# A selective-scan layer over image lines: step-size stores in slot 1, the gate behind the next turn's first scan, and another spread of B's units over VectorE and GpSimd

## The chip, the core and the metric

The kernel runs on one core of a Trainium2 chip. Times are device microseconds (us) of that core. The engines are TensorE (PE; its weight loads are listed as PEld), VectorE (DVE), ScalarE (ACT), GpSimd (POOL) and SyncE (SP), whose queue issues all the DMAs. Each engine works through its own queue in the order of the program, and waits for the others by semaphores.

## The reference, cut to what matters

Four residual layers follow one another on eight images of 48 x 48 pixels with 96 channels: a scan over the whole image in four directions (layer 0), a spectral layer (1), a scan over single lines in four directions (2, "lines"), and a second scan over the whole image (3). The change is in the lines layer, and in one helper that the two image scans also call. For each of its four directions lines computes

```python
xz = x @ in_w
xi = silu(conv4(xz[..., :192]) + conv_b)        # causal, 4 taps along the line
dt_low, Bm, Cm = split(xi @ xproj_w, [6, 22])
dt = softplus(dt_low @ dt_w + dt_b)             # step sizes
h = exp(dt * A) * h + (dt * xi) * Bm            # per channel and state, 16 states
y = (h * Cm).sum(states) + D * xi
y = y * silu(xz[..., 192:])                     # the gate
out += y @ outp_w @ out_w
```

with 192 inner channels in two halves of 96. A line is 48 pixels, and h starts from zero on each.

## The kernel before

**Blocks, slots, turns.** Each image and direction is cut into five blocks of lines: four of 10 lines (480 columns) and one of 8 (384 columns). Lines has 8 x 4 x 5 = 160 blocks. In a block there are 192 x 16 = 3072 pairs of channel and state, which lie on 128 partitions as 24 units of one block's columns each. Eight slots of three units make up the block: slots 0 to 3 belong to channel half 0, 4 to 7 to half 1, in the state order 0 1 2 3 3 2 1 0 (`ORDER`), so that slot 3 and slot 4, 2 and 5 and so on share B and C. Two slots make a turn; a block has four turns, q = 0 to 3, with at = 2 * (turn number).

**One turn in `scans`** (the loop from line 377), per engine in program order:

- DVE: `scan` of units 0 and 1; `make_dbu(at + 2)`, the product of dt * xi with B for the units of a slot of the *next* turn that lie on DVE; `scan` of units 2 and 3; `make_dbu(at + 3)`; `scan` of units 4 and 5; then `finish(at + 1)`.
- POOL: `make_hc(t - 1, 1)`, the product of the states with C for the second slot of the turn before; the units of `make_dbu(at + 2)` and `(at + 3)` that lie on POOL; `make_hc(t, 0)`.
- ACT: `make_da` (exponentials into PSUM, two buffers, two units each), `copy_b` of B for slots at + 3 and at + 4 into the one PSUM buffer that DVE reads, and what the block's preparation needs.
- PE: `reduce(t - 1, 0)` and `reduce(t - 1, 1)`, which sum over the states into the tile y. y has one PSUM bank. The first reduction of a half begins with an "opening" matmul that writes D * xi there, so it needs the bank free. After the last of a half, the pair (block, half) goes into the list `ends`.

`aside(at)` and `aside(at + 1)` stand in the middle and at the end of the turn. They issue, in this order, the loads of bc (B and C, slots 2, 3, 6, 7, for the next block) and of dd (step sizes dt and products dt * xi, slots 3 and 5, one channel half each, for the next block), a piece of side work, the preparation steps of `stage1` for later blocks, and the steps in `later`.

`finish` takes what lies in `ends` and calls `done` for it (line 838): DVE multiplies y by silu(z) into `gated` (the gate, line 843), which frees the bank. After the second half it books two steps, `project` (two matmuls with the output weights, line 852) and `add` (DVE adds into x, lines 858 and 860). Half 0 ends in turn 2, half 1 in turn 0 of the next block.

**Preparation of a block** (`stage1` of lines, from line 764). In the block two ahead of it: convolution of half 0 in slot 3 and of half 1 in slot 4 (PE, line 780), silu (ACT) and the x_dbl matmuls (PE, line 797) in slot 6, the copy of their result, B, C and dt_low, to `bcl` (ACT) and the dt matmuls (PE, line 808) in slot 7. In the block just before it: store of B and C and softplus in slot 0 (`s6`); matmuls for z and `make_du` (POOL, dt * xi) in slot 1 (`s7`); silu of z and the store of dd's half 0 in slot 2 (`s8`); the store of half 1 in slot 3. Stores go to DRAM (`store_dd`, line 437), because the loads read each row back on four partitions at once (`load_dd`, line 219).

**Spread.** `ON_POOL_L2` says how many of a slot's three units POOL multiplies with B; DVE has the rest. A slot with 3 there needs no copy of B in PSUM.

`make_du` (line 447) works on one half at a time in both kinds of scan layer. In the image scans (`ss2d`) it runs in slot 7 of the block two ahead, and the two stores of dd follow in slots 0 and 1 of the block just before; there `finish(at + 1)` and its place stay as they are (`restart` is False there and True in lines).

Of the kernel before, what the change touches and what calls it, by code (L numbers as in the profile page):

```python
# [23 lines left out]
SEG = 48  # L24
# [16 lines left out]
CH = 96  # L41

ON_POOL_SS = {2: 1, 3: 3, 5: 1, 6: 1, 7: 3}
ON_POOL_L2 = {3: 2, 5: 3, 6: 1, 7: 3}


DIRS_SS = [(False, False), (True, False), (False, True), (True, True)]
# [50 lines left out]
def vss_stack_kernel(ctx: ExitStack, tc: tile.TileContext, i: dict, out: bass.AP):  # L98
# [89 lines left out]
    def scans(dirs, order, restart, on_pool, a, pools, ps, stage1, opening, done, side, tail):  # L188
# [91 lines left out]
        def make_da(t, pair):  # L280
            if t >= nt:
                return
            b, q = turns[t]
            da = ps("da", 2, 1024)
            das[t, pair] = da
            for u in (2 * pair, 2 * pair + 1):
                half, sg = ORDER[2 * q + u // 3]
                ci = half * 12 + sg * 3 + u % 3
                at = (u - 2 * pair) * b.m
                nc.scalar.activation(da[:, at:at + b.m], b.got[half][:, u % 3, 0, :], AF.Exp, scale=a[:, b.k, ci:ci + 1])  # L290
# [86 lines left out]
        for t, (b, q) in enumerate(turns):  # L377
            at, nblk = 2 * t, t // (NG // 2)
            if q == 0:
                if nblk + 3 < len(blocks):  # L380
                    plan(blocks[nblk + 3], at + NG)
                if b.k == order[0] and b.first:
                    beside = side(b.job)
            scan(t, 0)
            if t > 0:
                make_hc(t - 1, 1)
            make_dbu(at + 2, nc.vector)
            make_da(t, 1)
            make_dbu(at + 2, nc.gpsimd)
            make_dbu(at + 3, nc.gpsimd)  # L390
            if t > 0:
                reduce(t - 1, 0)
            scan(t, 1)
            make_da(t, 2)
            copy_b(at + 3)
            make_dbu(at + 3, nc.vector)
            if t > 0:
                reduce(t - 1, 1)
            aside(at)
            begin(t + 2)  # L400
            make_hc(t, 0)
            make_da(t + 1, 0)
            scan(t, 2)
            copy_b(at + 4)
            finish(at + 1)
            aside(at + 1)
            if q == NG // 2 - 1 and b.k == order[-1] and b.last:
                for _ in beside:
                    while tail:
                        tail.pop(0)()  # L410
# [33 lines left out]
        b.room = pools["dds"].tile([DH, LEAD + 4 * WMAX], F32, tag="dds", name="dds")  # L444
        b.dds = b.room[:, LEAD:LEAD + 4 * b.m].rearrange("p (h t m) -> p h t m", h=2, t=2)

    def make_du(b, half, u):


        n = b.n  # L450
        dt, du = sizes(b, half)
        nc.gpsimd.tensor_mul(rows(du, n), rows(dt, n), u)  # L452
        if b.m == b.n:
            at = SEG - 1 if b.rev else 0
            nc.gpsimd.memset(rows(dt, n)[:, :, at:at + 1], FAR)
        elif half == 0:

            far = b.dds[:, :, :, b.came:] if b.back else b.room[:, :4 * b.m].rearrange("p (u m) -> p u m", m=b.m)[:, :, :LEAD + 1]
            nc.gpsimd.memset(b.dds[:, :, :, 0:1] if b.back else b.dds[:, :, :, b.goes:], 0.0)
            nc.gpsimd.memset(far, FAR)  # L460


    def ss2d(l, xin, xout, b0=0):
# [169 lines left out]
        def stage1(b):  # L633
            n = b.n
            u = b.view(us[b.job], dirs[b.k][0])
            got = {}

            def raw(half):
                got["p"] = ps("s1", 1)
                nc.tensor.matmul(got["p"][:DH, :n], lhsT=dtw[2 * NS:, b.k, half, :], rhs=b.bcl[2 * NS:, :n],  # L640
                                 start=True, stop=True)

            def biased(half):
                nc.scalar.activation(sizes(b, half)[0], got["p"][:DH, :n], AF.Identity,  # L644
                                     bias=w[f"{l}_dtb"][:, b.k, half:half + 1])

            def s0():
                got["p"] = ps("s1", 1)
                for half in range(2):
                    nc.tensor.matmul(got["p"][:NBC, :n], lhsT=w[f"{l}_xp"][:, b.k, half, :], rhs=u[:, half],  # L650
                                     start=(half == 0), stop=(half == 1))

            def s1():
                b.bcl = pools["bcl"].tile([NBC, BMAX], F32, tag="bcl", name="bcl")
                nc.scalar.copy(b.bcl[:, :n], got["p"][:NBC, :n])

            def s3():
                nc.sync.dma_start(b.bcd, b.bcl[:2 * NS, :n])
                raw(0)

            def s4():
                make_room(b, pools)
                biased(0)
                raw(1)

            def s6():
                both = b.dds[:, :, 0, b.at]
                nc.scalar.activation(both, both, AF.Softplus)  # L668

            def du():  # L670
                for half in range(2):
                    make_du(b, half, u[:, half])

            def store(half):
                return lambda: store_dd(b, half)

            return {-1: s0, 1: s1, 3: s3, 4: s4, 5: lambda: biased(1), 6: s6, 7: du,
                    NG: store(0), NG + 1: store(1)}

# [27 lines left out]
    def lines(xin, xout):  # L707
# [56 lines left out]
        def stage1(b):  # L764
            n = b.n
            col, rev = dirs[b.k]
            xp = xpads[b.job % 2]
            got = {}

            def shifted(off):  # L770
                v = shift(xp, off, 0).rearrange("p h w -> p w h") if col else shift(xp, 0, off)
                return v[:, b.r0:b.r0 + b.nr, :]

            def conv(half):
                def run():
                    got["u", half] = ps("s1", 2)
                    for tap in range(4):
                        off = tap - 3 if not rev else 3 - tap
                        at = ((b.k * 4 + tap) * 2 + half) * DH
                        nc.tensor.matmul(got["u", half][:, :n], lhsT=flat[:, at:at + P],  # L780
                                         rhs=shifted(off), start=(tap == 0), stop=(tap == 3))
                return run

            def s2():
                b.ub = up.tile([DH, 2, BMAX], F32, tag="ub", name="ub")
                for half in range(2):
                    nc.scalar.activation(b.ub[:, half, :n], got["u", half][:DH, :n], AF.Silu,
                                         bias=w["l2_cb"][:, b.k, half:half + 1])

            def s2s3():  # L790
                s2()
                s3()

            def s3():
                got["p"] = ps("s1", 2)
                for half in range(2):
                    nc.tensor.matmul(got["p"][:NBC, :n], lhsT=w["l2_xp"][:, b.k, half, :], rhs=b.ub[:, half, :n],
                                     start=(half == 0), stop=(half == 1))

            def s4():  # L800
                b.bcl = pools["bcl"].tile([NBC, BMAX], F32, tag="bcl", name="bcl")
                nc.scalar.copy(b.bcl[:, :n], got["p"][:NBC, :n])  # L802

            def s5():
                s4()
                for half in range(2):
                    got[half] = ps("s1", 2)
                    nc.tensor.matmul(got[half][:DH, :n], lhsT=dtw[2 * NS:, b.k, half, :], rhs=b.bcl[2 * NS:, :n],  # L808
                                     start=True, stop=True)

            def s6():
                nc.sync.dma_start(b.bcd, b.bcl[:2 * NS, :n])
                make_room(b, pools)
                for half in range(2):
                    nc.scalar.activation(sizes(b, half)[0], got[half][:DH, :n], AF.Softplus,  # L815
                                         bias=w["l2_dtb"][:, b.k, half:half + 1])

            def s7():
                for half in range(2):
                    got["z", half] = ps("s1", 2)  # L820
                    nc.tensor.matmul(got["z", half][:DH, :n], lhsT=w["l2_inz"][:, b.k, half * DH:(half + 1) * DH],  # L821
                                     rhs=shifted(0)[:C], start=True, stop=True)
                for half in range(2):
                    make_du(b, half, rows(b.ub[:, half], n))

            def s8():
                b.zb = up.tile([DH, 2, BMAX], F32, tag="zb", name="zb", bufs=2)
                for half in range(2):
                    nc.scalar.activation(b.zb[:, half, :n], got["z", half][:DH, :n], AF.Silu)
                store_dd(b, 0)  # L830

            return {3: conv(0), 4: conv(1), 6: s2s3, 7: s5, 8: s6, 9: s7, 10: s8, 11: lambda: store_dd(b, 1)}

        def opening(b, half):
            return diag[:, b.k, half, :], b.ub[:, half, :b.n]
# [3 lines left out]
        def done(b, half, y):  # L839
# [21 lines left out]
                if b.k == NK - 1 and b.last:  # L861
                    nc.sync.dma_start(xout[b.job], xs[b.job])

            return [(1, project), (2, add)]

        def side(job):
            if job + 1 < nb:
# [302 lines left out]
```

## Time and profile before

| | |
|---|---|
| median of 3 runs | 18718.93 us (18705.48 to 18734.97) |
| profiled execution | 18722.42 us, its span 18720.7 us |
| lines, first scan to last | 7024 to 13088 us of the span: 6064 us |
| DVE busy there | 5407 us, 3449 instructions |
| POOL / ACT / PE busy there | 4955 / 4706 / 5033 us |
| scan, 2 units of 480 columns (line 298) | 2146 ns on DVE |
| product with B, 3 / 2 / 1 units (line 266) | 1630 / 1127 / 629 ns on DVE |
| the same on POOL | 2738 / 1884 / 1035 ns |
| product with C, 3 units (line 304) | 2735 ns on POOL |
| make_du, one half (line 452) | 1031 ns on POOL |
| gate (line 843), addition (line 860) | 638 ns, 877 ns on DVE |
| loads of dd / bc, store of dd | 1440 / 480 / 360 KB each |

All rows but the first two are of 480 columns or of the stretch named. The busy time of an engine in a stretch says how much of it is work; a list of waits says which engine's instruction stood still and which event released it, with the total in us, the number of times, and the longest. The SP timeline gives the time at which a DMA is issued, not when it lands; landing shows where an instruction waits for it.

### The profile page before, as it was taken

The numbers are of one execution on the slowest core, as the hardware profiler recorded it, in microseconds if no ns is written. First come the engines' busy times: TensorE is split into PE (matmuls) and PEld (weight loads), VectorE is DVE, ScalarE is ACT, GpSimd is POOL, SyncE is SP. The second block draws the span as 40 slices with busy tenths as digits, with TensorE's granted clock in tenths as the row PEclk, the third lists the DMA queues.
The fourth block names the chain that finished last, engine by engine and source line by source line (L and its number), as shares of the span: only waits on it lengthen the run. The fifth ranks groups of instructions, "written<-read, shape, count | busy, mean of one in ns | idle before, by whom it ended". The sixth has DMA issues, their size and how long they took to land.

```text
span 18720.7 us, 168607 instructions
## 1 busy us (share of the span) xinstructions
PE 14799.0 (79%) x53500; PEld 4319.5 (23%) x53500; DVE 16219.3 (87%) x10329; ACT 13661.6 (73%) x20342; POOL 15238.6 (81%) x8639
## 2 busy tenths in 40 slices
PE   6777777777778887887888878878777777777777
PEld 1211211212215552222222222221121121121221
DVE  7999999999992218889898888888799999999998
ACT  6877877887772227777777777777687788778776
POOL 7999999999980008888888888888799999999998
PEclk7876787777767778888888888888677778778776
DMA  4544544544544334444444444343454554554444
GB/s 139 174 173 166 175 171 165 178 170 165 176 148 55 46 60 144 147 146 149 148 147 148 146 151 148 142 150 135 144 172 170 172 171 168 171 172 170 169 172 147
DMA packets 768455, 2836.52 MB, mean 152 GB/s; under 512 B 235724, under 2 KB 298668, under 8 KB 640926
## 3 DMA queue, kind: packets, MB, share of 16 engines
q1 hardware_dynamic: 767558, 2825.75, 45.0%
q8 instruction: 418, 6.85, 0.1%
q14 instruction: 479, 3.92, 0.1%
HBM read 2377.32 MB, written 448.17 MB: 151 GB/s over the span
## 4 chain that ended last, share of the span: by engine, by line
POOL 29%; DVE 16%; DMA 16%; PE 15%; issue 14%; ACT 9%; SPq 1%; POOLq 0%; DVEq 0%; ACTq 0%
POOL dbu L304 20%; DVE dbu L298 10%; DMA dd<-dds 8%; POOL dbu L266 6%; DMA bc<-bcd 6%; DVE dbu L266 4%; ACT ps_da L290 4%; PE ps_y L324 2%; POOL dds L452 2%; PE ps_h L1010 2%; PE ps_s L780 2%; PE ps_y L1023 2%; ACT L290 1%; PE ps_side L515 1%; PE ps_a L1000 1%
## 5 line engine op out<-in xcount | busy, mean ns | idle before, releaser
L298 DVE TENSOR_TENSOR_SCAN dbu<-ps_da,dbu 128x968 f32<-128x968 f32 (+3 forms) x5760 | 11814.6, 2074 | 615.1 <-ACT ps_da L290 511.7
L304 POOL TENSOR_TENSOR dbu<-dbu,bc 128x1440 f32<-128x1440 f32 (+1 forms) x3840 | 10062.3, 2633 | 1549.8 <-DVE dbu L298 1485.6
L290 ACT ACTIVATE ps_da<-dd,w_l_a 128x484 f32<-128x484 f32 (+3 forms) x11520 | 7429.8, 649 | 2970.4 <-DVE dbu L298 2732.3
L324 PE MATMUL ps_y<-dbu,w_red 128*32 128x480 f32 (+1 forms) x23040 | 4855.5, 736 | 2059.7 <-POOL dbu L304 2037.3
L326 PE MATMUL ps_y<-dbu,w_red 128*32 128x480 f32 (+1 forms) x7680 | 4814.4, 736 | 0.0
L266 DVE TENSOR_TENSOR dbu<-dd,ps_b 128x962 f32<-128x962 f32 (+5 forms) x2880 | 3831.1, 1330 | 387.8 <-ACT ps_b L247 353.1
L266 POOL TENSOR_TENSOR dbu<-dd,bc 128x481 f32<-128x481 f32 (+5 forms) x2240 | 3911.1, 1761 | 245.4 <-DMA bc<-bcd 136.7
L324 PEld LDWEIGHTS ps_y<-dbu,w_red 128*32 128x32 f32 x23040 | 743.5, 124 | 6084.7 <-POOL dbu L304 4390.8
L247 ACT COPY ps_b<-bc 128x482 f32<-128x482 f32 (+3 forms) x2720 | 1450.8, 533 | 463.4 <-DMA bc<-bcd 345.4
L780 PE MATMUL ps_s<-xpad,w_l_cw 128*128 128x480 f32 (+1 forms) x2560 | 1748.0, 835 | 2.2 <-ACT xpad L146 1.9
L515 PE MATMUL ps_side<-xpad,w_l_cw 128*128 128x480 f32 (+1 forms) x2880 | 1575.3, 676 | 17.7 <-ACT u L528 12.7
L290 ACT ACT_TABLE_LOAD x986 | 1265.0, 1283 | 17.4
L135 POOL MEMSET w_l_cw<- 128x1760 f32 (+1 forms) x3 | 5.8, 1941 | 1338.8 <-DVE x L990 1333.3
L320 PE MATMUL ps_y<-ysum,w_ident 96*96 96x480 f32 (+1 forms) x960 | 747.1, 867 | 285.7 <-ACT ysum L692 285.7
L452 POOL TENSOR_TENSOR dds<-dds,u 96x480 f32<-96x480 f32 (+1 forms) x640 | 764.7, 1195 | 207.2 <-ACT dds L668 181.6
L640 PE MATMUL ps_s<-bcl,dtw 6*96 6x480 f32 (+1 forms) x1280 | 867.0, 765 | 65.1 <-ACT dds L644 57.7
L650 PE MATMUL ps_s<-u,w_l_xp 96*38 96x480 f32 (+1 forms) x1280 | 843.4, 790 | 20.9 <-ACT z L530 17.9
L808 PE MATMUL ps_s<-bcl,dtw 6*96 6x480 f32 (+1 forms) x640 | 459.1, 859 | 500.1 <-ACT bcl L802 500.1
L515 PEld LDWEIGHTS ps_side<-xpad,w_l_cw 128*128 128x128 f32 x2880 | 581.7, 225 | 1067.7 <-issue 928.3
L780 PEld LDWEIGHTS ps_s<-xpad,w_l_cw 128*128 128x128 f32 x2560 | 513.9, 206 | 1070.0 <-issue 964.6
L326 PEld LDWEIGHTS ps_y<-dbu,w_red 128*32 128x32 f32 x7680 | 682.8, 124 | 0.0
L821 PE MATMUL ps_s<-xpad,w_l_inz 96*96 96x480 f32 (+1 forms) x640 | 504.0, 921 | 63.8 <-ACT dds L815 48.2
(147 smaller groups left out, 11829.0 us busy)
## 6 DMA issues: line engine op xcount, KB each, us to landing
dd<-dd SPq DMA_DIRECT2D x512, 1452.0 KB
bc<-bcd SPq DMA_DIRECT2D x1536, 480.0 KB
dd<-dd SPq DMA_DIRECT2D x256, 1440.0 KB
dd<-dds SPq DMA_DIRECT2D x512, 363.0 KB
dd<-dd SPq DMA_DIRECT2D x128, 1164.0 KB
bc<-bcd SPq DMA_DIRECT2D x384, 384.0 KB
dd<-dds SPq DMA_DIRECT2D x256, 360.0 KB
dd<-dd SPq DMA_DIRECT2D x64, 1152.0 KB
```

The lines of the kernel that those rows point to most:

```text
L247: nc.scalar.copy(bps[t][:, :bcs[t][0].shape[1]], bcs[t][0])
L266: engine.tensor_mul(o, du, by.unsqueeze(1).to_broadcast([P, hi - lo, by.shape[1]]))
L290: nc.scalar.activation(da[:, at:at + b.m], b.got[half][:, u % 3, 0, :], AF.Exp, scale=a[:, b.k, ci:ci + 1])
L298: nc.vector.tensor_tensor_scan(db, da, db, 0.0, ALU.mult, ALU.add)
L304: nc.gpsimd.tensor_mul(h, h, bcs.pop(2 * t + sub)[1].unsqueeze(1).to_broadcast([P, 3, n]))
L324: nc.tensor.matmul(y[32 * g:32 * g + 32, :n], lhsT=wc["red"][:, :32], rhs=hc[:, g, b.at], start=False, stop=(slot == 3))
L326: nc.tensor.matmul(y[DH:, :n], lhsT=wc["red"][:, 32:], rhs=hc[:, 2, b.at], start=(slot == 0), stop=(slot == 3))
L452: nc.gpsimd.tensor_mul(rows(du, n), rows(dt, n), u)
L515: nc.tensor.matmul(pu[:, :n], lhsT=flat[:, at:at + P], rhs=xpad[:, r0 + dy:r0 + dy + nr, dx:dx + W], start=(tap == 0), stop=(tap == 8))
L640: nc.tensor.matmul(got["p"][:DH, :n], lhsT=dtw[2 * NS:, b.k, half, :], rhs=b.bcl[2 * NS:, :n], start=True, stop=True)
L650: nc.tensor.matmul(got["p"][:NBC, :n], lhsT=w[f"{l}_xp"][:, b.k, half, :], rhs=u[:, half], start=(half == 0), stop=(half == 1))
L780: nc.tensor.matmul(got["u", half][:, :n], lhsT=flat[:, at:at + P], rhs=shifted(off), start=(tap == 0), stop=(tap == 3))
```

## The change

The spread of B's units in lines goes from slots 3, 5, 6, 7 with 2, 3, 1, 3 units on POOL to slots 1, 4, 5, 6, 7 with 1, 1, 3, 1, 3. In layers with `restart`, `finish` moves from the end of the turn to behind the first scan and the first product with B of the following turn; the steps that `done` books keep their slots, since their offsets shrink by one. `make_du` does both halves in one instruction, with one memset for both in lines. In lines both stores of dd are issued in slot 1 behind `make_du`, ahead of the loads of bc in slots 2 and 3 and of dd in slot 3, where they were behind the first of these and behind the first load of dd.

```diff
-ON_POOL_L2 = {3: 2, 5: 3, 6: 1, 7: 3}
+ON_POOL_L2 = {1: 1, 4: 1, 5: 3, 6: 1, 7: 3}
...
             make_dbu(at + 2, nc.vector)
+            if restart:
+                finish(at)
             make_da(t, 1)
...
             copy_b(at + 4)
-            finish(at + 1)
+            if not restart:
+                finish(at + 1)
             aside(at + 1)
...
-    def make_du(b, half, u):
-        n = b.n
-        dt, du = sizes(b, half)
-        nc.gpsimd.tensor_mul(rows(du, n), rows(dt, n), u)
+    def make_du(b, u):
+        dt, du = [b.dds[:, :, n, b.at].rearrange("p h (r s) -> p h r s", s=SEG) for n in range(2)]
+        nc.gpsimd.tensor_mul(du, dt, u)
         if b.m == b.n:
             at = SEG - 1 if b.rev else 0
-            nc.gpsimd.memset(rows(dt, n)[:, :, at:at + 1], FAR)
-        elif half == 0:
+            nc.gpsimd.memset(dt[:, :, :, at:at + 1], FAR)
+        else:
...
             def du():
-                for half in range(2):
-                    make_du(b, half, u[:, half])
+                make_du(b, u)
...
             def s7():
...
-                for half in range(2):
-                    make_du(b, half, rows(b.ub[:, half], n))
+                make_du(b, b.ub[:, :, :n].rearrange("p h (r s) -> p h r s", s=SEG))
+                for half in range(2):
+                    store_dd(b, half)

             def s8():
...
-                store_dd(b, 0)
-            return {3: conv(0), 4: conv(1), 6: s2s3, 7: s5, 8: s6, 9: s7, 10: s8, 11: lambda: store_dd(b, 1)}
+            return {3: conv(0), 4: conv(1), 6: s2s3, 7: s5, 8: s6, 9: s7, 10: s8}
...
-            return [(1, project), (2, add)]
+            return [(0, project), (1, add)]
```

## The prediction

> **What bounds the kernel now.** First the busy times by stage. The edited layer, called lines here, runs from its first scan at 7024 us to 13088 us, 6064 us of the 18720.7 us span. In the row below the busy columns are PE, PEld, DVE, ACT, POOL, then the granted clock, DMA share and GB/s.
>
> ```profile
> 7024.00:13088.00 6064.00, 5032.75 (x15976) 1330.59 (x15976) 5406.97 (x3449) 4706.10 (x6753) 4954.77 (x2556) 0.83 0.41 146
> ```
>
> VectorE (DVE) is busy 5407 us, 89%, so 657 us at most are to be had. Who ends its waits there:
>
> ```profile
> DVE dbu L298 <- ACT ps_da L290: 292.1, 300, 3.3
> DVE gated L843 <- PE ps_y L326: 155.4, 172, 5.4
> DVE dbu L266 <- ACT ps_b L247: 136.0, 88, 3.2
> DVE x L860 <- PE ps_s L852: 38.3, 46, 2.8
> ```
>
> Several engines end waits, so I ask what is late behind them. The waits of the SyncE queue (SP) have one big entry, and one block of its timeline shows the ring:
>
> ```profile
> SPq L219 <- DMA dd<-dds: 3008.9, 319, 11.3
> ```
>
> ```profile
> 10107.75 0.74 SPq L437 DMA_DIRECT2D dd<-dds  x1
> 10108.55 0.55 SPq L231 DMA_DIRECT2D bc<-bcd  x1
> 10117.88 0.51 SPq L219 DMA_DIRECT2D dd<-dd  x1
> 10118.50 0.73 SPq L437 DMA_DIRECT2D dd<-dds  x1
> 10129.65 0.53 SPq L219 DMA_DIRECT2D dd<-dd  x1
> 10130.23 1.24 SPq L231 DMA_DIRECT2D bc<-bcd  x2
> ```
>
> The first load of step sizes (dd) waits 10.1 us for store 0; store 1 sits behind it; the second load waits 11.2 us more; the loads of B and C (bc) that slot 2 of the next block needs come last. On DVE the two ends of that turn of the ring are
>
> ```profile
> 10099.85 1.66 DVE L266 TENSOR_TENSOR dbu<-dd,ps_b 128x1440 f32<-128x1440 f32 x1 [2.56 <-ACT ps_b L247]
> ```
> ```profile
> 10137.59 1.65 DVE L266 TENSOR_TENSOR dbu<-dd,ps_b 128x1440 f32<-128x1440 f32 x1 [0.99 <-ACT ps_b L247]
> ```
>
> From the first to store 0: 7.90 us; then 10.13, 0.62, 11.15, 0.58 and 7.36 us: 37.74 us. I measured this interval between slot-2 products over the layer: 111 of 480 columns after 480, mean 38.70 us (least 37.65); 16 from 480 to 384, 35.62; 16 from 384 to 384, 35.11; 16 from 384 to 480, 37.28. DVE itself needs only 34.7 us of a 480 block (12 scans at 2.07 from start to start, 15 of B's units 8.3, two gates 0.55, the addition 0.9). So a round trip through DRAM sets the period, and the other waits lie in its slack.
>
> **What the Trainium skill says.** "DMA: Bandwidth & Descriptors", section "Why a DMA increments its semaphore by 16 and not by 1": a transfer uses the largest number of engines up to 16 that divides the slowest dimension of both sides, and always the lowest-numbered ones. The store writes `j (g m) -> g j m` with g = 3, so three engines. The trace agrees: while only stores move (16017 to 16020 us), DMA share is 0.21, 0.20, 0.18 (3/16 is 0.19) at 74 to 85 GB/s. Same page, "Queues, rings and completion order": each engine takes descriptors in ring order. So whatever is issued behind a store waits behind it on those three engines; the scan layers confirm it below. "TensorE: Matmul & The Clock Gate", part 1: an idle window of about 3.4 us halves the clock until one busy window has passed. Here the clock goes to 0.50 at 10091 us after an idle stretch, and passes of 480 columns take 0.80 us instead of 0.41.
>
> **Part by part** (480 columns; against this execution, 18722.4 us with a span of 18720.7; the median of the runs, 18718.9, is 3.5 lower).
>
> *Spread of units.* DVE before: 4 x 1630 + 629 + 1127 = 8276 ns; after, 3 x 1630 + 3 x 1127 = 8271. POOL before: 1884 + 2738 + 1035 + 2738 = 8395; after, 3 x 1035 + 2 x 2738 = 8581. Zero in sum. It lengthens turn 0 on DVE by 1.0 us and shortens turn 3, so ScalarE's softplus with its two table loads (3.8 us) is covered better; 0 to 0.5 us a block. POOL has 32.1 of 34.7 us, and waits for scans where the 1.88 us leave.
>
> *du as one instruction.* POOL's 480, 960 and 1440 columns cost 1035, 1884, 2738 ns, so 960 cost about 1.9: 0.2 us of POOL saved. But store 0 left after the first half; now it leaves after both, about 0.75 us later: 7.90 + 0.75 = 8.65 us after slot 2's product. This is on the ring.
>
> *Stores at slot 1.* Store 0 had waited for POOL anyway and gains nothing. Store 1 passes a dd load and two bc loads, and these now stand behind it. Both scan layers issue just this: two stores, two bc, dd, dd. Their 156 pairs have the dd loads at +9.83 and +14.8 us (medians). So the second dd load starts 9.83 + 5.0 us after store 0 instead of 10.1 + 0.6 + 11.3 = 22.0: 7 us earlier, and the late bc load is gone. **But the first dd load lands later.** A case where DVE waited for it:
>
> ```profile
> 18499.57 1.84 SPq L437 DMA_DIRECT2D dd<-dds  x2
> 18501.51 3.19 SPq L231 DMA_DIRECT2D bc<-bcd  x2
> 18509.50 0.51 SPq L219 DMA_DIRECT2D dd<-dd  x1
> ```
> ```profile
> 18520.36 1.66 DVE L266 TENSOR_TENSOR dbu<-dd,ps_b 128x1443 f32<-128x1443 f32 x1 [0.76 <-DMA dd<-dd]
> ```
>
> Landing is 20.75 us after the stores. By the rate of the tail, 24 GB/s an engine: two stores 240 KB, two bc 60, the load's 90, together 390 KB in 16.2 us plus some 4.6 fixed: 20.8. In 384 columns 17.5 (estimate from the same sum).
>
> *The new ring.* From slot 2's product to store 0: 8.65. Landing: 20.75. Then slot 8's product (next block's slot 0) to the next slot-2 product: 1.65, the gate 0.6 (moved onto this stretch), scan 2.1, two units 1.05, scan 2.1, scan 2.15 = 9.65. **Sum 39.05 us**, 0.35 above today's mean. Without waits DVE would want dd 27.4 us after the block's start; it gets it at 31.4. For 480 to 384: 8.25 + 17.5 + 9.2 = 35.0; 384 to 384: 6.9 + 17.5 + 7.9 = 32.3; 384 to 480: 7.6 + 20.75 + 8.8 = 37.1.
>
> *Gates later.* DVE's own time is unchanged, and their wait (155 us) goes. Added: the next half's opening matmul needs the one y bank that the gate reads, and TensorE is in order. Behind it are both reductions, the projection and a convolution; DVE's addition, ACT's silu and the copy of bcl wait for those. In turn 1 the gate ends 4.1 us (two scans) ahead of the addition. Opening 0.9, two reductions 0.82 each, projection 1.65 and latency 0.25 make 4.4 us at full clock, 8.5 at half. TensorE idles 3 to 4 us before, so half clock at first: a wait of 0.3 to 4.3, I take 2.7. With 1.1 for scan 0 of turn 1 (it waits about 1.0 now) 3.8 us lie in the 4.0 us slack ahead of dd's landing: they cost nothing where that is late, and set the period (38.9) where it isn't. In turn 3 the gate comes after the landing, TensorE cold: opening, two reductions and x_dbl's matmuls end 7.9 to 10.7 us after slot 8's product begins, and ACT wants them at 8.05: 0 to 1.4 us on the ring, I take 0.3. In column directions convolutions cost 6.2 to 7.7 us a half, so the opening's delay reaches silu and scan 0: 0 to 1.3. With an ACT tie of 0.1, I add 0.65 in the mean: 39.7.
>
> *Sum.* 111 x (39.7 - 38.7) = +111. From 480 to 384 the waits of turn 1 have no cover: 38.1 against 35.6, 16 x 2.5 = +40. 384 to 384: 33.0, 16 x -2.1 = -34. 384 to 480: 37.5, +4. Lines: +121. The scan layers get the one-instruction du too: 0.2 us in each of 320 blocks of a POOL that runs beside a busier DVE (5172 against 5037 of 5421 us): -10, from -60 to +20. Total +111: 18722 + 111 less 3 is **18830**.
>
> **Rivals.** *A, the landing binds less than the sum says and the period falls to DVE's with TensorE's waits* (faster). Its place is slot 8's product: the period breaks even at a landing about 20.1 us after the stores (20.75 less the 0.65 of added waits), each us less comes off the ring, and from 16.7 on (27.4 less the 10.7 at which the stores go) it is gone. For it: no block of lines shows these stores together, and lines has less other traffic. Against: the 156 pairs are alike, and the case above is a wait seen, not a sum. Turn-1 waits of 0.3 to 2 us give 35.3 to 37.5 us a block, 111 x -2.3 and the rest alike, about -330: 18390; partly 18600. Chance 0.18. *B, it evens out*: the bare ring with no further wait gives 111 x 0.35 - 10 - 45 - 3 = -19, scan layers -10: 18690. Chance 0.17. *C, TensorE becomes the bound* (slower than forecast): half clock in turns 1 and 3 in most blocks, 40.6 us: 111 x 1.9 + 60 = +270: 18990. It decides from where gate to addition exceeds 8 us. Chance 0.15. *D, my forecast*, 18760 to 18910: 0.5. That the edit doesn't do what it says I can exclude only for store 0: it moves in slots, not in time.
>
> **Numbers.** A measurement tells 0.2% (37 us) from no change. Below 18681: A and a third of B: 0.23. Within: the rest of B and a little of D: 0.15. Above: 0.62. The range 18560 to 19010 leaves out A's full form and C's end.
>
> **What would show it.** Right: the two L437 together, dd loads at +9.8 and +14.8; "ACT ps_b L247 <- DMA bc" nearly gone; a new DVE wait of L266 on dd, some 2 to 4 us in most blocks; L843's wait gone and L320 waiting on gated; interval 39 to 40 us. Wrong: DVE not waiting for dd at slot 8, and an interval below 38.

## The result, and the profile after

The changed kernel takes 18895.2 us (median of 4 runs, 18881.8 to 18908.2) against 18717.8 (4 runs, 18705.5 to 18735.0): a ratio of 1.0094, 95% interval 1.0081 to 1.0106. It is slower by 177 us; the forecast was 111 slower. The profiled executions differ by 186 us (18908.2 against 18722.4), and the trace splits this into two parts of opposite sign. Lines, from its first scan to the end of its last, went from 6055 us (7024.0 to 13079.0; the 6064 us of the table of before run on behind the last scan) to 6292.6 us (7001.9 to 13294.5): **+237**. What lies before and behind it got **52 us shorter** (head 22, tail 30).

First the busy times of lines in the kernel after, in the same columns as the row shown of before (PE, PEld, DVE, ACT, POOL, clock, DMA share, GB/s).

```profile
7002.00:13294.00 6292.00, 5046.34 (x15952) 1303.62 (x15956) 5390.94 (x3447) 4707.36 (x6753) 4927.71 (x2396) 0.82 0.40 141
```

DVE has no more work, 5391 us against 5407, and TensorE hardly any, 5046 against 5033. On DVE all of the 237 us is waiting. Who ends DVE's waits in lines (total us, times, longest):

```profile
DVE x L861 <- PE ps_s L853: 372.0, 118, 4.0
DVE dbu L298 <- ACT ps_da L290: 308.5, 244, 5.5
DVE x L859 <- PE ps_s L853: 118.0, 40, 3.7
DVE dbu L266 <- DMA dd<-dd: 88.0, 73, 4.0
```

The gate's wait and the wait for B in PSUM, the second and third entry before, are gone. In their place stands the addition, which waits for TensorE's projection in 158 of 160 blocks: 372 + 118 = 490 us (L861 and L859). Before it waited 60 us: 38.3 in the row of L860 above, and in the blocks of the first direction

```profile
DVE x L858 <- PE ps_s L852: 21.8, 23, 2.1
```

The last row of the list after is new: it is the first dd load, for which DVE before waited once, 0.3 us.

The ring runs as the edit says. On SP:

```profile
SPq L219 <- DMA dd<-dds: 1338.6, 315, 5.9
```
```profile
10159.83 1.57 SPq L440 DMA_DIRECT2D dd<-dds  x2
10161.50 3.36 SPq L231 DMA_DIRECT2D bc<-bcd  x2
10169.48 0.51 SPq L219 DMA_DIRECT2D dd<-dd  x1
...
10174.16 0.51 SPq L219 DMA_DIRECT2D dd<-dd  x1
```

Both stores leave together, the two bc loads behind them, and the dd loads follow at +9.65 and +14.3 us. SP's wait fell from 3009 to 1339 us because a store no longer stands behind a waiting load. The landing, where DVE had to wait for it:

```profile
10181.37 1.66 DVE L266 TENSOR_TENSOR dbu<-dd,ps_b 128x1440 f32<-128x1440 f32 x1 [1.19 <-DMA dd<-dd]
```

That is 21.5 us after the stores here; over all 73 such waits the median is 20.75 us, with four fifths of them between 20.4 and 21.3.

Most of the time goes in turn 1 of a block. On DVE (start, duration, engine, line; in brackets the idle time just before and who ended it):

```profile
10119.97 2.16 DVE L298 TENSOR_TENSOR_SCAN dbu<-ps_da,dbu 128x960 f32<-128x960 f32 x1 [1.18 <-ACT ps_da L290]
10122.04 1.13 DVE L266 TENSOR_TENSOR dbu<-dd,ps_b 128x960 f32<-128x960 f32 x1
10123.09 0.64 DVE L844 TENSOR_TENSOR gated<-zb,ps_y 96x480 f32<-96x480 f32 x1
10123.65 4.19 DVE L298 TENSOR_TENSOR_SCAN dbu<-ps_da,dbu 128x960 f32<-128x960 f32 x2
10131.56 1.00 DVE L861 TENSOR_TENSOR x<-x,ps_s 96x480 f32<-96x480 f32 x1 [3.71 <-PE ps_s L853]
```

and on TensorE at the same time:

```profile
10123.79 1.92 PE L320 MATMUL ps_y<-ub,diag 96*96 96x480 f32 x2 [4.99 <-DVE gated L844]
10125.63 1.02 PE L324 MATMUL ps_y<-dbu,w_red 128*32 128x480 f32 x3
...
10128.99 2.52 PE L853 MATMUL ps_s<-gated,wo 96*96 96x480 f32 x4
```

The opening matmul (L320) stood 4.99 us until the gate had freed the bank of y. Only then come the reductions and, at 10128.99, the projection, which DVE's addition wants from 10127.85 on. From the gate's end at 10123.73 to the addition are 7.8 us, and DVE has two scans (4.2 us) to put there. In the windows below the first column after the length is PE's busy time, and the granted clock is the third from the end:

```profile
10121.00:10123.70 2.70, 0.00 (x0) 0.00 (x0) 2.70 (x4) 1.55 (x3) 2.70 (x3) 0.97 0.16 31
10123.70:10127.00 3.30, 3.21 (x10) 0.80 (x14) 3.30 (x3) 3.16 (x4) 3.30 (x2) 0.50 0.85 220
10127.00:10131.50 4.50, 4.50 (x17) 1.38 (x10) 0.84 (x1) 3.50 (x6) 4.50 (x2) 0.62 0.49 172
```

TensorE idles before the gate, and works behind it at half clock. The Trainium skill's "TensorE: Matmul & The Clock Gate", part 1, says that an idle window of about 3.4 us halves the clock, and the 4.99 us here are longer than that: wait and half clock are one effect, since the wait makes the idle stretch. It isn't this block alone: in the 3.3 us behind this gate the clock is 0.50 in the mean of the 160 blocks, where it was 0.81 before. Gate to addition is 7.1 us in the mean and 7.87 at most. By the prediction's sum, 4.4 us at full clock, the addition would wait some 0.3 us and not 3.1, so most of the wait would be the clock's; this is an estimate, and no run separates the clock from the delay.

Three more rows show what else stands behind the gates:

```profile
PE ps_y L320 <- DVE gated L844: 955.7, 239, 10.4
ACT ub L788 <- PE ps_s L781: 148.0, 63, 4.4
ACT L831 <- DVE gated L844: 38.2, 140, 0.5
```

TensorE's wait on the gate was this before:

```profile
PE ps_y L320 <- DVE gated L843: 53.9, 51, 7.2
```

ScalarE's silu of the convolutions (L788) waits for late convolutions, 148 us where it was 63, and only for blocks of the two directions that run over columns; scan 0 of the next turn 0 is late behind it. The silu of z (L831) now waits for the gate itself, whose input buffer it reuses.

DVE's sum closes: 34.7 us of work a block by the prediction's count, the addition 490/160 = 3.1, scan 0 of turn 0 189/160 = 1.2, scan 0 of turn 1 98/160 = 0.6, dd 88/160 = 0.55, together 40.1 us. Measured as in the prediction, from one slot-2 product to the next, 480 columns after 480, it is 40.16 us (before: 38.70).

### The profile page after: what moved, and what is told of

Same layout as the page of the kernel before. It is cut to its first block, busy times and chain, and to the rows that moved or that the text cites. A ratio compares the mean times of both kernels' runs of the same rounds, so it can differ in the third digit from the quotient of the medians.

```text
span 18906.4 us, 167818 instructions
## 1 busy us (share of the span) xinstructions
PE 14791.0 (78%) x53500; PEld 4281.4 (23%) x53500; DVE 16149.1 (85%) x10329; ACT 13659.3 (72%) x20342; POOL 15159.6 (80%) x8159
## 4 chain that ended last, share of the span: by engine, by line
POOL 27%; PE 21%; issue 16%; DVE 15%; DMA 11%; ACT 9%; SPq 0%; POOLq 0%; DVEq 0%; ACTq 0%
POOL dbu L304 18%; DVE dbu L298 9%; POOL dbu L266 6%; DVE dbu L266 5%; DMA dd<-dd 4%; PE ps_y L324 4%; PE ps_s L781 4%; DMA dd<-dds 4%; ACT ps_da L290 4%; POOL dds L454 3%; PE ps_h L1011 2%; PE ps_y L320 2%; PE ps_y L1024 2%; ACT L290 1%; DMA bc<-bcd 1%
## 5 line engine op out<-in xcount | busy, mean ns | idle before, releaser
L324 PE MATMUL ps_y<-dbu,w_red 128*32 128x480 f32 (+1 forms) x23040 | 4938.6, 753 | 1773.3 <-POOL dbu L304 1755.5
L326 PE MATMUL ps_y<-dbu,w_red 128*32 128x480 f32 (+1 forms) x7680 | 4900.6, 753 | 0.0
L266 DVE TENSOR_TENSOR dbu<-dd,ps_b 128x962 f32<-128x962 f32 (+7 forms) x2880 | 3831.6, 1330 | 373.2 <-ACT ps_b L247 223.0
L266 POOL TENSOR_TENSOR dbu<-dd,bc 128x481 f32<-128x481 f32 (+7 forms) x2400 | 3932.5, 1655 | 62.4 <-DMA bc<-bcd 36.5
L324 PEld LDWEIGHTS ps_y<-dbu,w_red 128*32 128x32 f32 x23040 | 785.2, 127 | 5847.5 <-POOL dbu L304 3847.5
L320 PE MATMUL ps_y<-ub,diag 96*96 96x480 f32 (+1 forms) x640 | 514.8, 902 | 955.7 <-DVE gated L844 955.7
L320 PE MATMUL ps_y<-ysum,w_ident 96*96 96x480 f32 (+1 forms) x960 | 754.7, 876 | 325.8 <-ACT ysum L693 325.4
L642 PE MATMUL ps_s<-bcl,dtw 6*96 6x480 f32 (+1 forms) x1280 | 880.5, 777 | 73.7 <-ACT dds L646 62.3
L454 POOL TENSOR_TENSOR dds<-dds,u 96x960 f32<-96x960 f32 (+1 forms) x320 | 707.0, 2209 | 184.4 <-ACT dds L670 184.4
L326 PEld LDWEIGHTS ps_y<-dbu,w_red 128*32 128x32 f32 x7680 | 721.3, 127 | 0.0
```

The source lines that it names most:

```text
L266: engine.tensor_mul(o, du, by.unsqueeze(1).to_broadcast([P, hi - lo, by.shape[1]]))
L320: nc.tensor.matmul(ys[b, half][:DH, :n], lhsT=lhsT, rhs=rhs, start=True, stop=False)
L324: nc.tensor.matmul(y[32 * g:32 * g + 32, :n], lhsT=wc["red"][:, :32], rhs=hc[:, g, b.at], start=False, stop=(slot == 3))
L326: nc.tensor.matmul(y[DH:, :n], lhsT=wc["red"][:, 32:], rhs=hc[:, 2, b.at], start=(slot == 0), stop=(slot == 3))
L454: nc.gpsimd.tensor_mul(du, dt, u)
```

## The experiments

Twelve more kernels, all times medians against the kernel before on the same chip. "Waits of DVE by place" means: in the trace's timeline of DVE, the idle time ahead of the instruction at one place in the turn, added up over the 160 blocks of lines.

| kernel | us | ratio to before (95%) |
|---|---|---|
| after | 18895.2 | 1.0094 (1.0081 to 1.0106) |
| after, gates back at the end of the turn | 18680.3 | 0.9980 (0.9973 to 0.9988) |
| after, addition later | 18848.7 | 1.0068 (1.0056 to 1.0081) |
| before, gates moved only | 18967.1 | 1.0134 (1.0120 to 1.0148) |
| before, stores and one du only | 18673.5 | 0.9976 (0.9967 to 0.9985) |
| after, only half 1's gate late | 18858.3 | 1.0074 (1.0062 to 1.0087) |
| after, only half 0's gate late | 18685.7 | 0.9984 (0.9976 to 0.9992) |
| gates back, wide stores in lines | 18381.6 | 0.9823 (0.9810 to 0.9837) |
| after, wide stores in lines | 18839.3 | 1.0063 (1.0049 to 1.0076) |
| before, wide stores in lines only | 18409.4 | 0.9834 (0.9821 to 0.9848) |
| gates back, wide stores everywhere | 18291.7 | 0.9773 (0.9759 to 0.9786) |
| before, new spread only | 18710.2 | 0.9998 (0.9989 to 1.0006) |
| stores, du, old spread, wide stores in lines | 18374.1 | 0.9816 (0.9803 to 0.9830) |

**My theory** after the result: the moved gate costs, over TensorE's in-order queue, and the ring through DRAM lies just under it. **The rival**: the ring is the cost (stores ahead of the loads land dd too late), and the waits for TensorE lie in its slack. A second one: the new spread.

### The gates back at the end of the turn

```diff
-            if restart:
-                finish(at)
...
-            if not restart:
-                finish(at + 1)
+            finish(at + 1)
...
-            return [(0, project), (1, add)]
+            return [(1, project), (2, add)]
```

> The changed kernel with the gates back at the end of the turn (project and add keep their slots); spread, one-instruction du and stores in slot 1 stay. Theory 'gate chain': the 3.1 us that the addition waits in nearly every block come from the late gate, so they go, and what is left is the ring through DRAM at 38.45 us (39.05 less the gate's 0.6) plus 0.4 of waits: lines from 6293 us to about 6090, total near 18715 (18680 to 18750), with DVE's wait for dd rising from 88 us to 200 or more. Rival 'ring alone': the late gate costs nothing, its wait only fills the slack ahead of dd: total stays within 40 us of 18895. Rival 'gate alone': the landing of dd does not bind, the period falls by the whole 3.1 us: near 18420.

Measured: 18680.3 us, at the lower edge of what was expected; lines 7007.8 to 13081.0, 6073 us, and 480 after 480 at 38.98 us. In lines DVE waits thus:

```profile
DVE dbu L266 <- DMA dd<-dd: 320.2, 133, 5.0
DVE dbu L298 <- ACT ps_da L290: 190.3, 288, 3.3
```

So the gate move costs 215 us in the presence of the other edits, and the rest of the change gains 37. The period of this kernel is the ring: 8.57 us from slot 2's product to the stores, 20.84 to slot 8's product, which waits for the landing in 108 of 111 blocks, and 9.57 to the next slot-2 product, in sum 38.98. The forecast's ring was 8.65 + 20.75 + 9.65 = 39.05, but its last term holds 0.6 us for the moved gate, which this kernel doesn't have there. In its place scan 0 of turn 0 waits for ScalarE; why is shown under "One gate at a time".

### The gate move alone, on the kernel before

```diff
+            if restart:
+                finish(at)
...
-            finish(at + 1)
+            if not restart:
+                finish(at + 1)
...
-            return [(1, project), (2, add)]
+            return [(0, project), (1, add)]
```

> The kernel before with nothing but the gates moved behind the next turn's first scan. Gate chain theory: the addition waits about 3 us in most blocks; the ring of before leaves DVE some 2 to 3 us of slack in that stretch, so a third to a half shows: near 18820 (18750 to 18900). Ring alone: the wait is hidden wholly, 18720 within 30, with the waits for late B gone instead.

Measured: 18967.1, above the range: 250 us slower than before, and 72 slower than the whole change. Lines takes 6312 us (7023.2 to 13334.8). The miss is informative: with the old order of stores I expected the old ring to hide more of the gate's delay. For a stretch of 5870 us of lines:

```profile
DVE dbu L298 <- ACT ps_da L290: 429.3, 247, 5.1
DVE x L863 <- PE ps_s L855: 294.5, 105, 3.7
DVE x L861 <- PE ps_s L855: 124.5, 40, 4.0
DVE dbu L266 <- ACT ps_b L247: 19.1, 11, 2.8
```

The late bc load (the wait for ps_b) bound the kernel before with 136 us in 88 waits, and here it has 11 left: the ring has slack, and TensorE's answer to the gate sets the period. The move needs no help from the stores to be slow.

### The stores and the one-instruction du alone, on the kernel before

```diff
-    def make_du(b, half, u):
+    def make_du(b, u):
...
             def s7():
...
+                for half in range(2):
+                    store_dd(b, half)
...
-                store_dd(b, 0)
```

> The kernel before with the one-instruction du and both stores in slot 1; gates and spread as before. If the landing of dd, 20.7 us after the stores, sets the period as the prediction had it, the ring is 38.45 us: lines within 60 us of before, the image scans some 50 us shorter: near 18690 (18640 to 18750), and DVE waits for dd in most blocks, 200 us or more in sum, for bc hardly at all. If dd's landing does not bind: near 18400. If moving the stores is what made the change slow: above 18800.

Measured: 18673.5. Lines is 6058 us, 3 more than before: the new ring replaces the old one at the same length. What is gained, 45 us by the profiles, lies outside lines (head 11, tail 33), where of this edit only the one-instruction du acts. Lines starts earlier in every kernel that has it (7012.6 us at the latest, against 7016.6 at the earliest in those without), though those without spread over 7 us among themselves.

### The new spread alone

> The kernel before with nothing but the new spread of B's units in lines. The ring of before (late B at slot 2) doesn't depend on it: 18718 within 35; the wait of scan 0 in turn 1 (157 us before) shrinks and the wait for late B grows by as much. If the spread is a gain by itself: below 18650.

The edit is the one line of `ON_POOL_L2`. Measured: 18710.2, no difference. It moves waits: scan 0 of turn 1 from 157 to 86 us, scan 0 of turn 0 from 108 to 189. So the second rival is out for the early gates; with the late ones the spread was not changed alone.

### One gate at a time

Half 1's gate late, half 0's as before:

```diff
-            if restart:
+            if restart and q == 1:
                 finish(at)
...
-            if not restart:
+            if not restart or q == 2:
                 finish(at + 1)
```

> The changed kernel with only the gate of half 1 late (turn 1 of the next block); the gate of half 0 is back at the end of turn 2. Theory: this gate makes the cost, since behind it stand the opening, two reductions, the projection for the addition, and the convolutions whose silu scan 0 of the next block waits for: the addition still waits about 3 us in nearly all blocks and the total stays at 18880 (18850 to 18910). Rival: the gate of half 0 costs as much (it lies on the ring and its matmuls end in x_dbl): near 18790.

Half 0's gate late, half 1's as before:

```diff
-            if restart:
+            if restart and q == 3:
                 finish(at)
...
-            if not restart:
+            if not restart or q == 0:
                 finish(at + 1)
...
-            return [(0, project), (1, add)]
+            return [(1, project), (2, add)]
```

> The changed kernel with only the gate of half 0 late (turn 3), the gate of half 1 back at the end of turn 0. Theory: 0.6 us on the ring in the 130 or so blocks in which dd binds, and little else: 18680 + 70 = 18750 (18720 to 18780), dd waits near 300 us. Rival: half of the gates' 215 us, 18790 or more.

Measured: 18858.3 with half 1's gate late, 18685.7 with half 0's. Against the kernel with both early (18680.3) that is 178 and 5 us; both late cost 215, and where the other 32 come from was not traced. For a stretch of lines, half 1's gate late:

```profile
DVE x L861 <- PE ps_s L853: 318.3, 110, 3.8
DVE dbu L266 <- DMA dd<-dd: 42.0, 40, 2.8
```

and half 0's late:

```profile
DVE dbu L266 <- DMA dd<-dd: 435.6, 136, 6.0
DVE dbu L298 <- ACT ps_da L290: 144.8, 216, 4.4
```

The first has the addition's wait and hardly one on dd; the second waits on dd in most blocks and is the ring. Half 0's gate was to lengthen that ring by its own 0.6 us (96 us over 160 blocks). It does lie on it, but scan 0 of turn 0, also on it, waits 50 us in place of 130. The traces show why. First the kernel with both gates early, from the landing of dd to the next slot-2 product, on DVE and on ScalarE:

```profile
9698.25 1.66 DVE L266 TENSOR_TENSOR dbu<-dd,ps_b 128x1440 f32<-128x1440 f32 x1 [2.17 <-DMA dd<-dd]
...
9705.73 2.16 DVE L298 TENSOR_TENSOR_SCAN dbu<-ps_da,dbu 128x960 f32<-128x960 f32 x1 [0.64 <-ACT ps_da L290]
9707.80 1.63 DVE L266 TENSOR_TENSOR dbu<-dd,ps_b 128x1440 f32<-128x1440 f32 x1
```
```profile
9699.94 0.56 ACT L247 COPY ps_b<-bc 128x480 f32<-128x480 f32 x1 [2.46 <-DVE dbu L266]
...
9704.33 1.36 ACT L290 ACTIVATE ps_da<-dd,w_l_a 128x480 f32<-128x480 f32 x2
```

and the same stretch on DVE with half 0's gate late:

```profile
9696.35 1.65 DVE L266 TENSOR_TENSOR dbu<-dd,ps_b 128x1440 f32<-128x1440 f32 x1 [4.04 <-DMA dd<-dd]
9697.92 0.64 DVE L844 TENSOR_TENSOR gated<-zb,ps_y 96x480 f32<-96x480 f32 x1
...
9701.60 4.38 DVE L298 TENSOR_TENSOR_SCAN dbu<-ps_da,dbu 128x960 f32<-128x960 f32 x2
9705.90 1.63 DVE L266 TENSOR_TENSOR dbu<-dd,ps_b 128x1440 f32<-128x1440 f32 x1
```

It takes 9.55 us in both (9.57 and 9.59 in the mean of 111 blocks). ScalarE can copy B only when slot 8's product has freed the PSUM buffer; then come two silus and the two exponentials of scan 0, with a table load of 1.28 us ahead of each pair, and they end 7.4 us after that product began. With the gate in its queue DVE reaches scan 0 at just that time; without it, DVE waits there. Half 0's gate lies in ScalarE's slack.

### The addition later, the gates left late

```diff
+            if restart and slot == 4:
+                for step in later.pop(at, []):
+                    step()
             run(at)
...
-            return [(0, project), (1, add)]
+            return [(0, project), (2, add)]
```

> The changed kernel, gates late as in it, but the addition into x one slot later (turn 2, ahead of that slot's convolution), so that DVE reaches it some 5 us later and TensorE's chain gate, opening, reductions, projection has time. Gate chain theory: the addition's wait (490 us in sum) goes nearly to zero; then the ring with the gate on it binds at 39.05 + 0.4, against 39.9 now: total near 18820 (18770 to 18860), dd waits rise to 250 or more. Ring alone: no change, 18895. Gate alone: near 18420.

The addition stands one slot further back on DVE. Measured: 18848.7, so only 46 of the 215 us come back, somewhat less than expected. For a stretch of lines:

```profile
DVE dbu L298 <- ACT ps_da L290: 442.4, 375, 6.1
DVE dbu L266 <- DMA dd<-dd: 328.6, 129, 5.0
```

The addition's wait is gone from DVE's list, and dd's takes its place (by place, 352 us in 137 blocks): the ring lies right behind. It is still longer than with the gates early. On its stretch from dd's landing to the next slot-2 product lie the gate of half 0 (0.6 us) and scan 0 of turn 0, which waits 201 us in place of 130 (0.44 a block): 1.04 x 160 = 167 us, against 168 measured between these two kernels. (For 480 after 480 the stretch itself grew from 9.57 to 10.52 us.) The close agreement is a sum, not a separate test. A new wait shows too: scan 0 of turn 2, 172 us in 158 blocks, behind the silu of z that waits for the gate; it comes before the landing and lies in its cover.

### The ring taken away

If the ring bounds the kernel with early gates, and the gate the kernel with late ones, a shorter ring must help the first and not the second. Each store is cut into three of 32 rows (`m` columns of dt and of du in a row):

```diff
     def store_dd(b, half):
+        if b.m == b.n:
+            for g in range(3):
+                nc.sync.dma_start(b.dd[half][:, 2 * g * b.m:2 * (g + 1) * b.m],
+                                  b.dds[32 * g:32 * (g + 1), half].rearrange("p t m -> p (t m)"))
+            return
```

> Gates back, and in lines each store of dd as three transfers of 32 rows, so that it is no longer spread over three DMA engines but over all. Ring theory: a store then moves 22 KB an engine instead of 120, lands in some 4 us, dd lands 10 us earlier, and DVE's wait for dd (320 us) goes; with the image scans untouched the total is near 18390 (18330 to 18460). Rival, the landing is set by something else than the three engines (DRAM, fixed latency, SP): dd waits stay above 200 us, total above 18600.

> The changed kernel with the same wide stores in lines, gates late. If TensorE's chain behind the gate sets the period by itself, only the 88 us of dd waits go: 18810 (18780 to 18850), the addition's wait stays near 490 us. If the ring sets it and the addition's wait is only slack: below 18600.

> The kernel before with nothing but the wide stores in lines (three transfers of 32 rows each, in their old slots). If the ring through the narrow stores is all that holds the kernel before, B is no longer late and lines falls as with the gates back and wide stores, less what the one-instruction du gave the image scans (about 50 us): near 18460 (18410 to 18520). If the place in slot 1 or the spread is needed as well: above 18560.

Measured: 18381.6 with early gates, 299 us less than with the narrow stores; 18839.3 with late gates, 56 less; 18409.4 on the kernel before, 309 less. The first came as expected, the second in the upper part of its range, the third at the lower edge of its own. SP with early gates:

```profile
10105.01 2.66 SPq L439 DMA_DIRECT2D dd<-dds  x6
10107.76 1.16 SPq L231 DMA_DIRECT2D bc<-bcd  x2
10109.09 1.20 SPq L219 DMA_DIRECT2D dd<-dd  x2
```

The dd loads leave from 4.1 us behind the stores on, in place of 9.65 and 14.3, with the same bytes. That is what the rule of the Trainium skill's "DMA: Bandwidth & Descriptors", section "Why a DMA increments its semaphore by 16 and not by 1", would have of it: the slowest dimension is now 32, which 16 divides, where it was 3. The trace agrees: in the 2.7 us from 10105 us on, in which the six stores are issued, DMA share is 0.65, and it was 0.18 to 0.21 while only narrow stores moved. DVE waits on dd no more, and is busy 5382 of lines' 5779 us, 93%. With late gates and the same stores, in a stretch of lines:

```profile
DVE x L866 <- PE ps_s L858: 342.0, 110, 3.9
DVE dbu L298 <- ACT ps_da L290: 334.4, 234, 5.5
DVE x L864 <- PE ps_s L858: 120.5, 40, 3.7
```

No dd row, the addition's wait unchanged (489 us by place, as in the kernel after), and 5.15 us of waits a block. The gate's chain sets this period with no ring at all. The rival, that the ring is the cost, falls: taking it away returns 56 of the 177 us. And the gate move, which costs 215 us beside the narrow stores, costs 458 beside the wide ones (18839.3 against 18381.6): so the ring had hidden more than half of it.

### The old spread with wide stores, and wide stores everywhere

The kernel with the gates back and wide stores in lines, with the line of `ON_POOL_L2` as before.

> As the version with the gates back and wide stores, with the old spread. With the ring gone the wait of scan 0 in turn 1 is no longer hidden: 60 to 100 us more than 18382, so near 18460. If the spread doesn't matter even there: 18382 within 30.

Measured: 18374.1, the same as with the new spread (18381.6) to within the measurement. I had expected the new spread to be worth 80 us once the ring was gone. It is worth nothing there either.

```diff
     def store_dd(b, half):
-        if b.m == b.n:
-            for g in range(3):
...
-            return
-        nc.sync.dma_start(b.dd[half].rearrange("j (g m) -> g j m", g=3), b.dds[:, half].rearrange("p t m -> p (t m)"))
+        for g in range(3):
+            nc.sync.dma_start(b.dd[half][:, 2 * g * b.m:2 * (g + 1) * b.m],
+                              b.dds[32 * g:32 * (g + 1), half].rearrange("p t m -> p (t m)"))
```

> As the version with the gates back and wide stores, with the wide stores in the image scans too. Their DVE hardly waits for dd, so nothing is to be had there: 18380 within 30. If the three engines hold them up as well, below 18330.

Measured: 18291.7, 0.9773 of before, the fastest of all and 88 us below the expected time, as was to be the case if the three engines held up the image scans too. The last image scan, first with narrow stores there, then with wide ones:

```profile
12766.00:18374.00 5608.00, 4303.58 (x15448) 1106.25 (x15444) 5233.45 (x3201) 4324.01 (x6531) 5106.90 (x2871) 0.74 0.50 167
```
```profile
12726.00:18288.00 5562.00, 4243.31 (x15444) 1092.02 (x15444) 5229.52 (x3200) 4321.17 (x6531) 5107.08 (x2871) 0.76 0.51 169
```

The same work in 46 us less; the first image scan gives 44 more. The loads' wait behind the stores on SP, 1039 us in the last scan, is gone, and DVE's waits there fall from 369 to 327 us, spread over many small ones. Which of them carries the gain was not settled.

## Why the prediction was right, and where it was mis-sized

The direction, the likeliest case and the bound before held. Sizes were off in both directions and partly cancel, and the cost was put on the wrong one of the two gates.

- **What bounds before: right.** Shortening the ring alone takes 309 us from the kernel before; the wait for B in PSUM goes with it, and those of the scans of turn 0 (108 us before and after) and of the addition (57 and 55) stay.
- **Spread: right.** Zero in sum, and zero on the chip (0.9998, interval 0.9989 to 1.0006).
- **Landing and new ring: right in size.** 20.75 us after the stores forecast, 20.75 measured in 73 waits. The du of 96 x 960 takes 1.88 us, forecast 1.9. The ring is 38.98 us with early gates, forecast 39.05 with the gate in it.
- **Which gate costs: wrong.** The forecast put half 0's gate on the ring, with its 0.6 us and 0.3 of waits behind it, and in blocks of 480 columns let the waits of turn 1, behind half 1's gate, lie in the cover of the landing. Alone, half 0's gate costs 5 us and half 1's 178. It is luck that the ring's sum came out all the same: what the gate was to add to it, ScalarE's wait fills with the gate or without.
- **Rival A** needed a landing under 20.1 us. None is seen: the least of the 73 waits is 20.14, and with the gates back, where 108 of 111 blocks of 480 after 480 wait, 20.24. **Rival B** had the ring bare of further waits, at 18690. The kernel with the gates back takes 18680.3, but it has a wait of ScalarE where B had a gate, so the agreement is in part chance. **Rival C** decides from gate to addition over 8 us; the most in 160 blocks is 7.87.
- **The signs.** The ring's order, the vanished waits and the new one of L320 came as forecast. The wait for dd did not: 2 to 4 us in most blocks were forecast, and it is 1.2 us in 73 of 160. With both gates early it is 2.4 us in 133. The interval, forecast at 39 to 40 us, is 40.16.

The intervals between slot-2 products, as in the prediction, in us:

| columns | times | before | forecast | measured | forecast in sum | measured in sum |
|---|---|---|---|---|---|---|
| 480 to 480 | 111 | 38.70 | 39.7 | 40.16 | +111 | +162 |
| 480 to 384 | 16 | 35.61 | 38.1 | 36.92 | +40 | +21 |
| 384 to 384 | 16 | 35.11 | 33.0 | 37.23 | -34 | +34 |
| 384 to 480 | 16 | 37.28 | 37.5 | 38.34 | +4 | +17 |

- **480 to 480, "I add 0.65 in the mean": too small, 1.1 over the ring's 39.05.** Turn 1 was well sized: the addition's wait 3.1 (forecast 2.7) and scan 0 of turn 1 0.6 (forecast 1.1) make 3.7 against 3.8. Scan 0 of turn 0 was left out of the chain. It waited before the change already, 108 us in 80 blocks. In the 64 of them that follow the convolutions of a column direction it waits 2.7 us now, and waited 1.45; the growth is at the upper end of the 0 to 1.3 forecast, but the chain's period of 38.9 held only turn 1's waits and turn 3's 0.3. With 1.2 us for this scan, the mean of all blocks, the chain is 34.7 + 3.1 + 0.6 + 1.2 = 39.6, longer than the bare ring's 39.05. So "they cost nothing where that is late" did not hold: behind such a chain DVE waits for the landing in only half of these blocks.
- **384 to 384: wrong.** I had let the shorter store win there. But no wait on dd is on a product of 384 columns; the addition waits 3.3 us in these blocks, as in the others, and the landing covers none of it. This is 68 us of the miss, the largest piece.
- **Scan layers: -10 forecast, -52 measured.** The range given for this term, -60 to +20, holds it. I had counted 0.2 us of POOL. The kernel with only stores and du confirms that it comes with the du (-45 outside lines); through which wait in the image scans was not traced.

In sum, lines was forecast +121 and came +237, the rest was forecast -10 and came -52. That the forecast of 18830 is only 65 below the measured 18895 owes something to these two misses going opposite ways. The sign and the cause hold: a ring that the edit makes hardly longer, and a gate that frees the one bank of y too late for TensorE, which works in order.

Three things stay open: which wait in the image scans pays for the one-instruction du and the wide stores, why both gates late cost 32 us more than each alone, and how much of the addition's wait is the half clock's.

## What to carry to other kernels

Before an instruction is moved later, ask which buffer it frees and what stands in order behind the one that wants it: here a 0.6 us multiplication, moved by one scan and one product, held up an opening matmul, two reductions and a projection, and TensorE, idle until then, did just that work at half clock. Where two chains have nearly the same length, add up each one whole, with the waits that are there already, and take the longer; a wait is in cover only if the other chain stays the longer after it. And look at how many DMA engines a store uses before moving it: cutting the same bytes into three stores of 32 rows was worth more (1.7%) than every reordering tried.

## What the runs showed of the hardware

The wide stores had been expected to help where DVE waited on dd. They also gained 90 us in the image scans, where DVE's wait on dd in the last one was only 11.7 us in all. And a bound can hide another almost whole: the same edit to the stores is worth 299 to 309 us with the gates early and 56 with them late. The reverse holds too: 0.6 us of DVE's work was put on the ring and cost 5 us in all, because ScalarE's copy, two silus and two exponentials with their two table loads took as long, 7.4 us from the product that frees B's buffer.
